# Turning layer 0's output through VectorE and DRAM, and a written order for three engines

## The chip, the cores and the metric

The kernel runs on one core of a Trainium2 chip. The metric is the device time of one execution in microseconds. A core has five engines with their own instruction streams: TensorE (PE: matmuls and transposes into PSUM; its weight loads are listed as PEld), VectorE (DVE), ScalarE (ACT), GpSimd (POOL) and SyncE (SP), which here only issues DMAs. The engines wait for one another through semaphores. A DMA's data is moved by 16 DMA engines that all issuing engines share.

## The reference

The input x has 128 graphs of 64 nodes with 256 features. Four layers follow; after each, its output is added to its input and a layer norm over the features is taken. One adjacency matrix (64 by 64) serves all graphs.

```
x = layernorm(x + L0(x))   # graph attention: Wh = x W; e = leaky(s1_i + s2_j), masked; softmax(e) Wh
x = layernorm(x + L1(x))   # GATv2 over 512 edges, 4 heads: leaky(Xq[src] + Xq[dst]) . a, softmax per src,
                           # sum of weights times Xv[dst], times W_out
x = layernorm(x + L2(x))   # normalised adjacency, two linear layers with batch norm over all rows
x = layernorm(x + L3(x))   # two graph convolutions, then four small LSTMs over windows of 1 to 4 nodes
```

The change touches layers 0 and 1 alone.

## The kernel before

**Tiling.** The 8192 rows are cut into 16 quarters (NQ) of 512 rows (QT), each of four tiles of 128 rows (PQ). A "token-major" tile has rows on the partitions, a turned one has features on the partitions; a matmul over features needs the turned one. The buffer A in SBUF has one slot of 128 by 1024 per quarter. In the old kernel it first takes layer 0's input squares, then layer 0's output (`token_major(q)`), and later layer 2's.

**Layer 0, steps per quarter.** `l0_a` gets the turned input: for quarter 0 by TensorE transposes, eight of them with two copies by ScalarE (`transposed`, lines 198 to 206), for the others by one VectorE transpose (line 220). That instruction only turns blocks of 32 by 32, so the input is loaded for it in such squares by eight DMAs of 64 KB (lines 131 to 135), with the squares at their turned places. `l0_b` projects (line 230), `l0_c` makes the scores and their exponentials (lines 241 to 252) and the reciprocal of the row sums (254), `l0_d` turns the weights, `l0_e` multiplies them with the values, adds x and takes the layer norm (lines 270 to 275): statistics on VectorE, then a power and four normalising instructions on GpSimd. The result goes into A.

**Layer 1.** `l1_t` turns that result with eight TensorE transposes (line 204) and two ScalarE copies (205). `l1_qv` makes queries and values in two halves (lines 295 to 308). `l1_graph`, eight per quarter, makes the edge sums (332) and a ReLU (334); `sums` reduces them over features (323). Two quarters share one softmax over edges (a super, S): `l1_softmax`, `l1_sums`, `l1_weights`. The last one writes the weights to a table in DRAM by four indirect DMAs from GpSimd (378), and two DMAs from SyncE load it back as dense attention matrices (384). `v_a` copies a quarter's part on GpSimd (391) and multiplies it with the values, `v_b` applies W_out, adds layer 0's result and normalises, `v_c` applies layer 2's adjacency.

**Order.** A loop over the quarters (lines 659 to 676) gives each iteration eight slots; slot b starts with `l1_graph(q, b)`, and a list `between` names the steps that follow in it. Steps of several quarters are in flight at once: layer 0 runs two quarters ahead, the values of layer 1 three or four behind. `step` ties TensorE's instructions of a step behind the last TensorE instruction of the step before (649). The order on the other engines, and on SyncE, is the planner's: it places what it takes to be ready, and each engine then works its list in order. The small set-up functions fill in during the first two iterations.

**Buffers.** Three PSUM banks named `m` serve nearly all steps; `z` has two double banks, and the head sums one.

Of the kernel before, what the change touches and what calls it, by code (L numbers as in the profile page):

```python
# [41 lines left out]
def kernel(ctx: ExitStack, tc: tile.TileContext, i, out):  # L42
# [69 lines left out]
    with ExitStack() as two:  # L112
# [13 lines left out]
        def load_x(q):  # L126
            xin[q] = xp.tile([P, PQ, D], F32, name="xin")
            nc.sync.dma_start(xin[q], x_view[q])
            if q:

                rows = i["x"][q * QT:(q + 1) * QT, :].rearrange("(j t) (k i f) -> i k t j f", t=32, k=KD, f=32)
                for n in range(4):
                    for k in range(KD):
                        to = A[n * 32:(n + 1) * 32, q, k * QT:(k + 1) * QT]
                        nc.sync.dma_start(to.rearrange("t (j f) -> t j f", f=32), rows[n, k])

        class su:

# [27 lines left out]
        for s in range(2):  # L166
            nc.sync.dma_start(bd[s * N:(s + 1) * N, s * N:(s + 1) * N], i["adj"])
        load_x(1)

        wq = wa.tile([P, KD, D + HEADS], F32, name="wq")  # L170
        wv = wa.tile([P, KD, D], F32, name="wv")
# [42 lines left out]

        def l0_a(q):
            L0[q] = {"x": xin.pop(q)}
            if q:

                L0[q]["xT"] = work.tile([P, KD, QT], F32, name="tT", bufs=1)
                nc.vector.transpose(L0[q]["xT"].rearrange("p k t -> p (k t)"), A[:, q, :])  # L220
            else:
                L0[q]["xT"] = transposed(L0[q]["x"], q)

        def l0_b(q):
            xT = L0[q]["xT"]
            wh = L0[q]["wh"] = own(q, [P, PQ, D + 2], "wh")
            for c in range(PQ):
                p_ = bank([D + 2])
                for k in range(KD):
                    nc.tensor.matmul(p_, xT[:, k, c * P:(c + 1) * P], w0[:, k, :],  # L230
                                     start=k == 0, stop=k == KD - 1)
                nc.scalar.activation(wh[:, c, :], p_, AF.Copy)

            sb = L0[q]["sb"] = own(q, [P, PQ, P], "sb")
            nc.scalar.activation(sb, wh[:, :, D + 1:].to_broadcast([P, PQ, P]), AF.Copy)

        def l0_c(q):
            wh, sb = L0[q]["wh"], L0[q]["sb"]
            sc = bank([PQ, P])
            for c in range(PQ):  # L240
                nc.tensor.transpose(sc[:, c, :], sb[:, c, :], ident)
            e = L0[q]["e"] = work.tile([P, PQ, P], F32, name="e0")
            for c in range(PQ):
                nc.vector.scalar_tensor_tensor(e[:, c, :], sc[:, c, :], wh[:, c, D:D + 1], mask,
                                               op0=OP.add, op1=OP.add)
            nc.vector.scalar_tensor_tensor(e, e, SLOPE, e, op0=OP.mult, op1=OP.max)
            mx = small.tile([P, PQ], F32, name="mx")
            nc.vector.tensor_reduce(mx, e, AX.X, OP.max, negate=True)
            sm = small.tile([P, PQ], F32, name="sm")
            for c in range(PQ):  # L250
                nc.scalar.activation(e[:, c, :], e[:, c, :], AF.Exp, bias=mx[:, c:c + 1],
                                     accum_out=sm[:, c:c + 1])
            ri = L0[q]["ri"] = small.tile([P, PQ], F32, name="ri")
            nc.vector.reciprocal(ri, sm)

        def l0_d(q):
            e = L0[q]["e"]
# [4 lines left out]
            nc.scalar.activation(eT, p_, AF.Copy)  # L262

        def l0_e(q):
            x, wh, eT, ri = (L0[q][n] for n in ("x", "wh", "eT", "ri"))
            for c2 in range(2):
                p_ = bank([2, D])
                for c in range(2):
                    g = 2 * c2 + c
                    nc.tensor.matmul(p_[:, c, :], eT[:, g, :], wh[:, g, :D], start=True, stop=True)  # L270
                for c in range(2):
                    g = 2 * c2 + c
                    nc.vector.scalar_tensor_tensor(x[:, g, :], p_[:, c, :], ri[:, g:g + 1], x[:, g, :],
                                                   op0=OP.mult, op1=OP.add)
            layernorm(token_major(q), x, PQ, nc.gpsimd)
            L0.pop(q)
            if q + 2 < NQ:
                load_x(q + 2)

# [1 line left out]
        L1 = {}  # L281

        def l1_t(q):
            L1[q] = {"xT": transposed(token_major(q)), "qs": [],
                     "v": vp.tile([P, PQ, D], F32, name="v", bufs=5)}

        def l1_qv(q, c2):
            xT, v = L1[q]["xT"], L1[q]["v"]

            sp = spads[q // BPS % 2].rearrange("p (s e x b d h) -> p s e x b d h", e=2, s=2, x=2, b=BPS, d=2)  # L290
            pv = bank([2, D])
            for c in (2 * c2, 2 * c2 + 1):
                pq = bank([D + HEADS])
                for k in range(KD):
                    nc.tensor.matmul(pq, xT[:, k, c * P:(c + 1) * P], wq[:, k, :],  # L295
                                     start=k == 0, stop=k == KD - 1)
                for k in range(KD):
                    nc.tensor.matmul(pv[:, c % 2, :], xT[:, k, c * P:(c + 1) * P], wv[:, k, :],  # L298
                                     start=k == 0, stop=k == KD - 1)

                qs = work.tile([P, 2, D], F32R, name="qs", bufs=6)
                L1[q]["qs"].append(qs)
                for s in range(2):
                    r, ro = slice(s * N, (s + 1) * N), slice((1 - s) * N, (2 - s) * N)
                    nc.scalar.activation(qs[r, s, :], pq[r, :D], AF.Copy)  # L305
                    nc.vector.tensor_sub(qs[ro, s, :], pq[r, :D], qs[r, s, :].bitcast(F32))  # L306
                    nc.scalar.activation(sp[r, s, c % 2, 0, q % BPS, c // 2, :], pq[r, D:], AF.Copy, scale=SLOPE)
            nc.scalar.activation(v[:, 2 * c2:2 * c2 + 2, :], pv, AF.Copy)
# [30 lines left out]
        def l1_softmax(S):  # L339

            pe = pes.pop(S)
            nc.tensor.matmul(pe, spads[S % 2], gath, start=False, stop=True)
            e = vp.tile([P, E], F32, name="e1")
            nc.vector.tensor_add(e, pe, lb)
            up = vp.tile([P, E], F32, name="up")
            dn = vp.tile([P, E], F32, name="dn")


            nc.vector.tensor_tensor_scan(up, seg[:, :E], e, NEG, OP.add, OP.max)
            nc.vector.tensor_tensor_scan(dn[:, ::-1], seg[:, 1:][:, ::-1], up[:, ::-1], NEG, OP.add, OP.max)  # L350
            nc.vector.tensor_sub(e, e, dn)
            nc.scalar.activation(e, e, AF.Exp)
            sm[S] = e, up, dn

        def l1_sums(S):
            e, up, dn = sm[S]
            nc.vector.tensor_tensor_scan(up, keep, e, 0.0, OP.mult, OP.add)
            nc.vector.tensor_tensor_scan(dn[:, ::-1], seg[:, 1:][:, ::-1], up[:, ::-1], NEG, OP.add, OP.max)

# [24 lines left out]
                nc.sync.dma_start(ld[S][s * N:(s + 1) * N], half)  # L384


        def v_a(q):
            S, b = divmod(q, BPS)
            v = L1[q]["v"]
            am = vp.tile([P, PQ * HEADS, N], F32, name="am")  # L390
            nc.gpsimd.tensor_copy(am.rearrange("p (e r) n -> p e r n", e=2),
                                  ld[S].rearrange("p n (e b r) -> p b e r n", e=2, b=BPS)[:, b])
            pY = [bank([KD, PQ, N]) for _ in range(2)]
            for c in range(PQ):
                for h in range(HEADS):
# [242 lines left out]
        LAG = BPS + 1  # L638


        queue = []

        def step(do, n, *more):
            if not 0 <= n < NQ:
                return
            traced = nc.cur_bb.bb.instructions
            first = len(traced)
            if queue:
                with tc.issue_after(queue[-1]):
                    do(n, *more)  # L650
            else:
                do(n, *more)
            mine = [t for t in traced[first:] if t.engine == mybir.EngineType.PE]
            queue.extend(mine[-1:])

        def sums(q):
            reduce_heads([pend.pop(0) for _ in range(min(4, len(pend)))])
# [1 line left out]
        for q in range(NQ):  # L659
            S = q // BPS - 1 if q % BPS == 0 else -1  # L660
            between = [
                [(l0_e, q + 1), (l0_a, q + 2)],
                [(sums, q if q else -1), (l1_softmax, S)],
                [(l1_sums, S), (l0_b, q + 2)],
                [(v_b, q - LAG - 1)],
                [(l1_weights, S), (l1_t, q + 1), (l0_c, q + 2)],
                [(sums, q), (l1_qv, q + 1, 0)],
                [(v_c, q - LAG - 1), (v_a, q - LAG)],
                [(l0_d, q + 2), (l1_qv, q + 1, 1)],
            ]  # L670
            for b in range(GQ):
                step(l1_graph, q, b)
# [62 lines left out]
        q = 0  # L735
        for do, n in [(v_b, NQ - LAG - 1), (v_c, NQ - LAG - 1)] + [
                (do, n) for n in range(NQ - LAG, NQ) for do in (v_a, v_b, v_c)]:
            do(n, *[False] * (do == v_c))
            up_block(q)
            q += 1  # L740
# [397 lines left out]
```

## Time and profile before

| | |
|---|---|
| Time, median of 3 runs | 2139.26 us (2139.17 to 2140.81) |
| The profiled execution | 2138.25 us, span 2136.4 us |
| TensorE, VectorE, ScalarE, GpSimd busy | 96%, 41%, 44%, 20% |
| Layers 0 and 1 in the loop | from about 53 to 522 us of the span |
| One even and the next odd iteration there | 32.7 and 28.5 us |
| TensorE transposes of layer 0's output, of the layer's 16 quarters | 128 (line 204), about 0.27 us each, overlapping |
| DMA engines' share in an odd iteration | 0.51 |

An even iteration (q even, from 2) has the three steps of a softmax in it, an odd one has not. Times in the profile are microseconds from the start of the span. A line of a timeline gives the start, the length, the engine, the source line, the instruction and its tiles, how many were merged, and in brackets how long the engine had been idle before it and what released it. Matmuls overlap their neighbours, so the cost of one is read from the start of one to the start of the next.

### The profile page before, as it was taken

How to read it: one execution, taken by the hardware profiler on the slowest of the kernel's cores; microseconds unless marked ns; L12 is line 12 of the kernel's file. 1: busy time of each engine (PE TensorE's matmuls, PEld its weight loads, DVE VectorE, ACT ScalarE, POOL GpSimd, SP SyncE). 2: the span in 40 equal slices, each digit the busy share in tenths (PEclk: the TensorE clock that was granted, in tenths of full speed). 3: DMA queues.
4: the chain of work that ended last, by engine and by line, in shares of the span. 5: the costliest groups of instructions: out<-in, count | busy, mean ns of one | idle time of the engine just before them, and what ended most of it. 6: DMA issues, size and time to landing. Idle time of an engine off the chain costs nothing.

```text
span 2136.4 us, 29441 instructions
## 1 busy us (share of the span) xinstructions
PE 2060.7 (96%) x11343; PEld 1330.1 (62%) x11343; DVE 885.9 (41%) x2069; ACT 932.1 (44%) x1795; POOL 430.1 (20%) x569
## 2 busy tenths in 40 slices
PE   5999999998999989999999999999999999999998
PEld 4666767665544444585576576577467468468467
DVE  7456566654444343333234334324324324323213
ACT  2776666664339014334234334334334334333333
POOL 1134334332210010121112112113103103102012
PEclk8999999998999989999999999999999999999999
DMA  5244532322240021012112102103103102101001
GB/s 144 63 69 73 85 61 53 52 43 43 43 118 29 0 89 60 21 54 66 40 46 74 40 29 90 40 11 99 50 6 104 50 1 89 50 1 60 20 1 60
DMA packets 232636, 113.41 MB, mean 53 GB/s; under 512 B 150192, under 2 KB 215728, under 8 KB 232240
## 3 DMA queue, kind: packets, MB, share of 16 engines
q1 hardware_dynamic: 230640, 109.57, 20.2%
q8 instruction: 89, 1.46, 0.3%
q0 software_dynamic: 1024, 1.05, 0.2%
q10 hardware_dynamic: 832, 0.92, 0.1%
q14 instruction: 51, 0.42, 0.1%
HBM read 67.45 MB, written 44.04 MB: 52 GB/s over the span
## 4 chain that ended last, share of the span: by engine, by line
PE 86%; DVE 6%; ACT 4%; issue 2%; POOL 1%; DMA 1%; SPq 0%; POOLq 0%; DVEq 0%; ACTq 0%
PE l L994 36%; PE l L1000 20%; PE pz L784 5%; PE pz L719 5%; PE e L323 3%; PE g L933 2%; PE g L945 2%; PE m L295 2%; PE m L230 2%; PE z L332 2%; PE m L298 2%; PE g L878 1%; PE m L413 1%; PE m L270 1%; ACT u L334 1%
## 5 line engine op out<-in xcount | busy, mean ns | idle before, releaser
L994 PE MATMUL l<-H,wih 128*128 128x256 f32 (+2 forms) x2496 | 787.5, 470 | 1.8 <-ACT H L957 1.2
L994 PEld LDWEIGHTS l<-H,wih 128*128 128x128 f32 x2496 | 471.4, 190 | 286.2 <-issue 185.6
L1000 PE MATMUL l<-hid,whh 128*128 128x256 f32 (+2 forms) x1536 | 435.9, 437 | 0.0
L1000 PEld LDWEIGHTS l<-hid,whh 128*128 128x128 f32 x1536 | 291.8, 190 | 128.4 <-issue 61.2
L1006 ACT ACTIVATE gate_i<-l,bias 128x256 f32<-128x256 f32 (+2 forms) x176 | 100.3, 570 | 441.9 <-PE l L1000 374.2
L1010 POOL TENSOR_TENSOR cell<-gate_f,cell 128x256 f32<-128x256 f32 (+2 forms) x96 | 85.0, 885 | 726.0 <-ACT gate_f L1006 726.0
L1009 DVE TENSOR_TENSOR gate_i<-gate_i,gate_g 128x256 f32<-128x256 f32 (+2 forms) x96 | 49.6, 517 | 415.1 <-ACT gate_g L1006 415.0
L83 POOL TENSOR_TENSOR ln_rs<-ln_rs,mhalf 128x2 f32<-128x2 f32 (+2 forms) x97 | 82.0, 846 | 571.6 <-DVE ln_rs L95 570.7
L334 ACT ACTIVATE u<-z 128x1024 f32<-128x1024 f32 x128 | 130.3, 1025 | 63.3 <-PE z L332 62.3
L1006 ACT ACTIVATE gate_g<-l,bias 128x256 f32<-128x256 f32 (+2 forms) x176 | 100.3, 570 | 107.9 <-PE l L994 59.5
L1014 ACT ACTIVATE gate_g<-cell 128x256 f32<-128x256 f32 (+2 forms) x176 | 90.0, 511 | 86.9 <-DVE cell L1013 45.0
L1013 DVE TENSOR_TENSOR cell<-gate_i,gate_g 128x512 f32<-128x512 f32 (+2 forms) x80 | 48.2, 602 | 186.5 <-ACT gate_g L1006 186.4
L1006 ACT ACTIVATE gate_o<-l,bias 128x256 f32<-128x256 f32 (+2 forms) x176 | 99.3, 564 | 59.9 <-PE l L1000 54.0
L719 PE MATMUL pz<-A,w 128*128 128x512 f32 x256 | 113.1, 595 | 0.0
L332 PE MATMUL z<-gath_r,qs 128*128 128x512 f32 x256 | 100.4, 480 | 0.7 <-ACT u L334 0.4
L306 DVE TENSOR_TENSOR qs<-m,qs 64x256 fp32r<-64x256 f32 x128 | 54.0, 422 | 107.0 <-ACT qs L305 104.8
L719 PEld LDWEIGHTS pz<-A,w 128*128 128x128 f32 x256 | 47.9, 190 | 55.3 <-issue 53.3
L295 PE MATMUL m<-wq,tT 128*128 128x260 f32 x256 | 71.8, 403 | 7.8 <-ACT yT L403 5.4
L1006 ACT ACTIVATE gate_f<-l,bias 128x256 f32<-128x256 f32 (+2 forms) x96 | 51.1, 532 | 59.6 <-PE l L1000 59.1
L1023 DVE TENSOR_TENSOR hid<-gate_o,gate_g 128x256 f32<-128x256 f32 (+2 forms) x96 | 47.4, 493 | 61.2 <-ACT gate_o L1006 35.1
L721 DVE BATCH_NORM_STATS2 st<-pz 128x6 f32<-128x512 f32 x64 | 44.4, 697 | 59.5 <-PE pz L719 59.4
L1023 DVE TENSOR_TENSOR H<-gate_o,gate_g 128x512 f32<-128x512 f32 (+1 forms) x64 | 41.3, 645 | 66.6 <-PE l L994 46.1
(242 smaller groups left out, 2525.2 us busy)
## 6 DMA issues: line engine op xcount, KB each, us to landing
way<-st SPq DMA_DIRECT2D x59, 256.0 KB
st<-way SPq DMA_DIRECT2D x236, 64.0 KB
xin<-in_x SPq DMA_DIRECT2D x16, 512.0 KB
ld<-table SPq DMA_DIRECT2D x16, 512.0 KB
x_dram<-y SPq DMA_DIRECT2D x16, 512.0 KB
x2r<-x_dram SPq DMA_DIRECT2D x32, 256.0 KB
x_dram<-A SPq DMA_DIRECT2D x64, 128.0 KB
x3r<-x_dram SPq DMA_DIRECT2D x64, 128.0 KB
```

Of the source, the lines that this page charges most:

```text
L83: nc.gpsimd.tensor_tensor(dst, dst, mhalf[:, :n], OP.pow)
L295: nc.tensor.matmul(pq, xT[:, k, c * P:(c + 1) * P], wq[:, k, :], start=k == 0, stop=k == KD - 1)
L332: nc.tensor.matmul(z[:, k, :], L1[q]["qs"][c][:, s, k * P:(k + 1) * P], gath_r, start=True, stop=True)
L334: nc.scalar.activation(u, z, AF.Relu)
L719: nc.tensor.matmul(p_, w1[:, k, m * P:(m + 1) * P], A[:, q, k * QT:(k + 1) * QT], start=k == 0, stop=k == KD - 1)
L784: nc.tensor.matmul(p_, w2[:, k, m * P:(m + 1) * P], hidden(q, k), start=k == 0, stop=k == M1 - 1)
L994: nc.tensor.matmul(gates[n], wih[p][:, k, mw * P:(mw + 1) * P], Hw[:, k, :, s, :], start=k == 0, stop=not s and k == KD - 1)
L1000: nc.tensor.matmul(gates[n], whh[p][:, k, m * P:(m + 1) * P], hid[:, k], start=False, stop=k == KD - 1)
L1006: nc.scalar.activation(act[n], gates[n], AF.Tanh if n == "g" else AF.Sigmoid, bias=bias[:, p - 1, m:m + 1])
L1010: nc.gpsimd.tensor_tensor(cell[:, j], act["f"], cell[:, j], OP.mult)
L1014: nc.scalar.activation(act["g"], cell[:, j], AF.Tanh)
L1023: nc.vector.tensor_mul(Hw[:, jj, :, s, :] if over else new[:, jj], o, t)
```

## The change

Layer 0's output is no longer turned by TensorE for quarters 2 to 15. `l0_e` writes it to a buffer in DRAM, reads it back in 32 by 32 squares with eight DMAs, and `l1_t` turns it with one VectorE transpose. Quarters 0 and 1 (`TURN = 2`) are turned by TensorE in both layers, so quarter 1's input goes back from VectorE to TensorE. The slots of A are used for more: the squares of quarter q+1's input are loaded into A once `l0_b(q)` has read what stood there, and layer 0's squares of x1 follow in the same slot.

The list of steps is new, and `step` now ties the instructions of TensorE, VectorE and GpSimd each behind the last one of the same engine in the step before. Layer 0 finishes at the end of an iteration (slot 7) and not at the start; the second half of the queries stands in slot 0 of its own quarter's iteration; the copy of the attention weights is a step of its own, `v_am`. The exponential of layer 1's softmax moves from `l1_softmax` to `l1_sums`, behind the ScalarE instructions traced by then. Layer 0's reciprocal moves from `l0_c` to `l0_e`.

```diff
+        TURN = 2
+        def load_squares(to, rows):
...
+        def load_xT(q):
+            load_squares(A[:, q, :], i["x"][q * QT:(q + 1) * QT, :])
...
         def l0_a(q):
-            if q:
-                L0[q]["xT"] = work.tile([P, KD, QT], F32, name="tT", bufs=1)
-                nc.vector.transpose(L0[q]["xT"].rearrange("p k t -> p (k t)"), A[:, q, :])
-            else:
+            if q < TURN:
                 L0[q]["xT"] = transposed(L0[q]["x"], q)
+                return
+            t = A[:, q + 1, :] if q + 1 < NQ else work.tile([P, KD * QT], F32, name="tT", bufs=1)
+            nc.vector.transpose(t, A[:, q, :])
+            L0[q]["xT"] = t.rearrange("p (k t) -> p k t", k=KD)
...
             nc.scalar.activation(sb, wh[:, :, D + 1:].to_broadcast([P, PQ, P]), AF.Copy)
+            if TURN <= q + 1 < NQ:
+                load_xT(q + 1)
...
             layernorm(token_major(q), x, PQ, nc.gpsimd)
+            if q >= TURN:
+                x1 = dram.tile([QT, D], F32, name="x1_dram", bufs=2)
+                nc.sync.dma_start(x1.rearrange("(c p) d -> p c d", p=P), token_major(q))
+                sq[q] = A[:, q + 1, :] if q + 2 < NQ else xp.tile([P, PQ, D], F32, name="xin").rearrange(
+                    "p c d -> p (c d)")
+                load_squares(sq[q], x1)
...
         def l1_t(q):
-            L1[q] = {"xT": transposed(token_major(q)), "qs": [],
...
+            xT = work.tile([P, KD, QT], F32, name="tT", bufs=1)
+            nc.vector.transpose(xT.rearrange("p k t -> p (k t)"), sq.pop(q))
...
+            with tc.issue_after([t for t in nc.cur_bb.bb.instructions if t.engine == mybir.EngineType.Activation][-1]):
+                nc.scalar.activation(e, e, AF.Exp)
...
+            for t in traced[first:]:
+                if t.engine in (mybir.EngineType.PE, mybir.EngineType.DVE, mybir.EngineType.Pool):
+                    latest[t.engine] = t
...
             between = [
-                [(l0_e, q + 1), (l0_a, q + 2)],
-                [(sums, q if q else -1), (l1_softmax, S)],
-                [(l1_sums, S), (l0_b, q + 2)],
-                [(v_b, q - LAG - 1)],
-                [(l1_weights, S), (l1_t, q + 1), (l0_c, q + 2)],
+                [(l0_e, -1 if q else 1), (l0_a, -1 if q else 2), (l1_qv, q if q else -1, 1)],
+                [(sums, q if q else -1), (l1_softmax, S), (l0_b, q + 2)],
+                [(l1_sums, S), (v_b, q - LAG - 1)],
+                [(l0_c, q + 2), (l1_t, -1 if q else 1), (v_am, q - LAG)],
+                [(l1_t, q + 1 if q else -1), (l1_weights, S)],
                 [(sums, q), (l1_qv, q + 1, 0)],
-                [(v_c, q - LAG - 1), (v_a, q - LAG)],
-                [(l0_d, q + 2), (l1_qv, q + 1, 1)],
+                [(l0_d, q + 2), (v_c, q - LAG - 1)],
+                [(v_a, q - LAG), (l0_a, q + 3 if q + 4 < NQ else -1), (l0_e, q + 2),
+                 (l0_a, q + 3 if q + 4 == NQ else -1)],
             ]
```

## The prediction

> **What bounds the kernel now.** I read the page first, then the layer 0/1 stage cut into quarter-loop iterations (the `for q` loop; I call its odd and even passes iterations), then each engine's timeline over two of them, then SyncE's and GpSimd's timelines and the DMA share in short windows.
>
> The page's first section, two of its groups, and the table by stage (columns: length; busy TensorE, weight load, VectorE, ScalarE, GpSimd; granted clock; DMA share; GB/s):
>
> ```profile
> PE 2060.7 (96%) x11343; PEld 1330.1 (62%) x11343; DVE 885.9 (41%) x2069; ACT 932.1 (44%) x1795; POOL 430.1 (20%) x569
> ...
> L204 PE MATMUL m<-ident,A 128*128 128x128 f32 x64 | 9.5, 279 | 5.4 <-ACT tT L205 2.8 <-issue 2.7
> ...
> L220 DVE STREAM_TRANSPOSE tT<-A 128x1024 f32<-128x1024 f32 x7 | 8.7, 1245 | 0.2
> ...
> 283.50:316.20 32.70, 30.23 (x276) 21.94 (x274) 23.11 (x53) 20.75 (x46) 12.55 (x14) 1.00 0.13 37
> 316.20:344.70 28.50, 27.98 (x266) 20.97 (x265) 14.32 (x43) 20.14 (x45) 10.87 (x12) 1.00 0.51 75
> ...
> 478.00:482.00 4.00, 1.64 (x10) 1.43 (x10) 3.91 (x7) 1.06 (x2) 0.36 (x1) 0.87 0.00 0
> 482.00:485.00 3.00, 2.31 (x11) 1.81 (x9) 3.00 (x11) 0.80 (x2) 0.09 (x1) 0.50 0.00 0
> ```
>
> TensorE bounds the stage: idle 2.47 us in an even iteration (q=8, with a softmax in it) and 0.52 in an odd one. The last two rows show an idle stretch being followed by half clock. Now the timelines of TensorE and VectorE in the odd iteration, then SyncE and GpSimd:
>
> ```profile
> 325.53 3.61 PE L413 MATMUL m<-wout,yT 128*128 128x256 f32 x16
> 328.80 0.82 PE L332 MATMUL z<-gath_r,qs 128*128 128x512 f32 x2
> ...
> 332.94 0.69 DVE L248 TENSOR_REDUCE mx<-e 128x4 f32<-128x512 f32 x1
> ...
> 302.29 1.09 POOL L378 DMA_INDIRECT table<-at,place  x1 [7.61 <-DVE ln_rs L95]
> ...
> 314.12 0.96 POOL L378 DMA_INDIRECT table<-at,place  x1 [2.73 <-DMA table<-at,place]
> 316.27 3.23 SPq L384 DMA_DIRECT2D ld<-table  x2
> ...
> 319.00:321.00 2.00, 2.00 (x18) 0.42 (x16) 2.00 (x7) 1.02 (x1) 0.00 (x0) 1.00 1.63 132
> ...
> 326.48 1.98 POOL L391 COPY am<-ld 128x1024 f32<-128x1024 f32 x1 [1.07 <-DMA ld<-table]
> ...
> 1014.51 0.34 SPq L863 DMA_DIRECT2D way<-st  x1
> 1016.54 2.46 SPq L865 DMA_DIRECT2D st<-way  x4
> ```
>
> See three things. VectorE finishes layer 0's scores (L248) at 333.63, that is 4.83 us after TensorE left the v_b step (L413, 328.80). The attention table takes 14.0 us from the first indirect write to the issue of its load (302.29 to 316.27), and the load 10.2 more to land (316.27 to 326.48) with the DMA engines full. The last pair is layer 3's own turn through DRAM: the reads go out 2.03 us after the write.
>
> **The Trainium skill.** VectorE: DVE Perf Modes, "The three transpose paths", says that VectorE turns 32x32 blocks only; the trace agrees in so far as L220 needs eight DMAs to place the squares first. DMA: Bandwidth & Descriptors, "Queues, rings and completion order", says that all DMAs issued by SyncE use one row of rings and that each engine takes descriptors in ring order; here the table load fills the engines from 318 to 326, and I have no case of overtaking. The same page, "Two DMAs through the same engine are not ordered", says that a DMA reading what another wrote must be issued after that one's semaphore; L865 does wait. TensorE: Matmul & The Clock Gate, "Part 1", puts the clock at half after an idle window of about 3.4 us; the 0.50 at 482 to 485, after a wait of 2.25 us and shorter ones, agrees roughly.
>
> **What is removed.** For q = 2 to 15, eight transposes (L204) and two ScalarE copies (L205, 598 ns). On TensorE, start to start, eight cost 0.88 us in the odd iteration (329.45 to 330.33), 1.30 in the even one. If every wait went too, a pair of iterations would gain 0.88 + 0.52 + 1.30 + 2.47 = 5.2 us. For ScalarE, 1.2 us per quarter is free: it is 71% busy. Quarter 1 goes back from VectorE to TensorE: eight transposes more, but the start is VectorE-bound (its L220 at 23.66 is on the chain just before the projection at 24.96), so I take a gain of 3 us (0 to 4).
>
> **What is added on VectorE.** 14 transposes of 1.25 us. VectorE is only 50 to 71% busy, but now its order is written out, and the new one stands behind layer 0's scores and in front of the query matmuls.
> Odd iteration: xT is ready 4.83 + 1.25 = 6.1 us after v_b. TensorE has in between three graph steps (0.66 each), L241 (0.4) and the sums (1.86): 4.2. It waits 1.9 us. The rest of the old iteration without transposes and wait is 28.5 - 0.88 - 0.52 = 27.1; with the 1.9, and 0.4 for layer 0's last matmuls, which now need a bank just behind v_a, 29.4 against 28.5: +0.9.
> Even iteration: VectorE's chain from the softmax's first add (289.42) to the end of the scores (305.20) is 15.8 us, and holds everything that now precedes the query matmuls' banks, the reciprocal L372 too. Add the transpose (1.25) and 0.7, since the exponential now stands behind a ReLU on ScalarE: 17.7. The softmax matmul ends 7.3 us into the new iteration (graph step 0.66, second half of queries and values 3.55 as at 341.17 to 344.72, graph step 0.66, sums 1.86, L342 0.56), so the banks are free near 25.3. About 2.3 of query and value matmuls and 6.0 for the last two slots follow: 33.6 against 32.7, so +0.9.
> The six full pairs (q = 2 to 13) thus lose 6 x 1.8 = 11 us, though 5.2 each were taken off TensorE. The ends give back: 3 at the start, 0.9 in iteration 1, 3 in iteration 14 (L204 there runs in the half clock). Sum: +4.
>
> **What is added in transfers.** Per quarter a write of 512 KB and eight reads of 64 KB in 128-byte pieces; layer 0's own eight stay but come just in time (20 us ahead of their use, hidden). x1 is ready 6.9 us after layer 0's first add (318.47 to 325.40 in the trace). With a free queue: write about 3 (2.03 for 256 KB in layer 3, so an estimate), eight issues 4.1 (0.43 to 0.58 each), landing 1.6 after the last issue (in layer 3, 936.33 to the reader's start at 937.96). That is about 15.7 us after the iteration's start, and the transpose's turn is at 18.9 (v_b ends at 14.1, plus 4.83). Hidden, with 3 us to spare, when the iteration is even.
> In front of an odd iteration it isn't free. Weights are ready about 26 into the even iteration of about 34; 14.0 later, 6 into the odd one, the table load is issued. It lands at 16.2. x1 is ready near 8.2 (its normalisation stands behind the last indirect write on GpSimd), its write is issued at 9.3 behind the load's two issues and moves its data behind the load: landed near 18.1. Reads out at 22, landed at 23.5. VectorE waits 4.6 us in its in-order queue; behind it are the query differences (L306), and TensorE waits for these. With the 1.9 above, TensorE is idle over 6 us, so the clock halves; I take 1.5 us (0 to 3.4) for it. Six times 6.1 is 36.6. I take it, since SyncE really sat before this load in the old trace, from 187.2 (its previous issue) to 193.62: the order on SyncE puts the load early.
>
> **Moved at no cost.** The reciprocal (178 ns) waits for nothing at its new place. The copy of the attention weights on GpSimd (L391, 1.99) moved a slot ahead of v_a: the table has landed by then (16.2 against 19.7). Load of x for q+2: needed a whole iteration later. Writes of x2 (2 us of DMA): their reader is layer 3.
>
> **Sum.** 4 + 36.6 = 40.6 us on the profiled span of 2136.4. The timed runs have a median of 2139.26, so I forecast 2139.3 + 40.6, near 2180 us.
>
> **Rivals.**
> 1. The transfer hides (24%). x1's write and squares pass before or between the table load's packets. For it: the odd stretch has DMA share 0.51, so there is room on average. Against: the share is 1.63 exactly while the load runs. Then +4: 2143, spread 2135 to 2153.
> 2. Faster (28%). One mechanism: TensorE keeps the 5.2 us of a pair, because the turned tile is ready before TensorE reaches the query matmuls, in slot 5. The point: VectorE must be done within 4.2 us of v_b, where I count 6.1. It needs the layer norm of v_b or the scores to start earlier than traced, for instance because v_b's second half is reached sooner. Full price: -6 x 5.2 - 7 = -38; half of it, as I think likelier, -19: 2120, spread 2101 to 2134. For it: VectorE has 14 us idle in an odd iteration (28.5 less 14.32). Against: the 4.83 us are contiguous work.
> 3. Worse (6%). The next quarter's layer 0 squares, ready 10.2 us into the iteration, are issued while SyncE waits for x1's write, and their 4.1 us of data go first: another 4.1 x 6 = 25, so 2205.
> Nothing suggests that the change would not do what it says: fourteen quarters lose L204.
>
> **How the numbers follow.** My case has 42%, its own range 2163 to 2196. Slower is 42 + 6 + 16 (of rival 1); within 0.2%, 4.3 us and about what can be told from no change, 8 of rival 1; faster 28. The range 2112 to 2198 leaves out about 7 below and 7 above.
>
> **What would show it.** L204 at 16 transposes for layer 0 and 16 for layer 1; VectorE's new transpose at about 1.25 us, waiting for the DMA of the squares for some 4 to 5 us in odd iterations and hardly in even ones; SyncE issuing x1's write behind the table load; the query matmuls (L295's successor) waiting 6 us in odd iterations, 2 to 4 in even ones; clock 0.5 after the odd waits; layers 2 and 3 unchanged in length. I am wrong if the squares land before 18.9 in odd iterations, or if the pair is under 61 us.

## The result and the profile after

| | before | after |
|---|---|---|
| Time, median | 2139.22 us (4 runs, 2138.34 to 2140.81) | 2177.14 us (4 runs, 2174.45 to 2179.53) |
| Ratio | | 1.0176, 95% interval 1.0158 to 1.0194 |
| Span of the profiled execution | 2136.4 us | 2173.8 us |

The change made the kernel 37.9 us slower. The first section of the page, the groups of the new transpose and of what is left of the old one (part of a grouped view up to 560 us), and two iterations, q=10 and q=11, as a table of windows with the columns of before:

```profile
PE 2062.7 (95%) x11239; PEld 1325.8 (61%) x11239; DVE 899.7 (41%) x2082; ACT 919.6 (42%) x1769; POOL 414.9 (19%) x569
```

```profile
L310 DVE STREAM_TRANSPOSE tT<-A 128x1024 f32<-128x1024 f32 x12 | 14.9, 1241 | 9.4 <-DMA A<-in_x 9.4
L214 PE MATMUL m<-ident,A 128*128 128x128 f32 x16 | 3.6, 350 | 0.8 <-ACT lb L639 0.8
```

```profile
375.10:409.70 34.60, 31.24 (x269) 22.32 (x267) 23.42 (x54) 19.92 (x44) 12.31 (x15) 0.95 0.34 80
409.70:440.60 30.90, 27.52 (x257) 19.95 (x256) 15.84 (x44) 19.31 (x43) 9.13 (x12) 1.00 0.68 121
...
396.00:400.00 4.00, 1.93 (x5) 1.26 (x6) 3.93 (x6) 1.72 (x9) 4.00 (x5) 0.80 0.25 99
400.00:402.00 2.00, 2.00 (x6) 1.62 (x6) 1.35 (x5) 0.85 (x3) 1.12 (x2) 0.55 0.20 74
```

The transposes are gone as announced: 16 instructions of L214 on A are left, those of quarters 0 and 1, and VectorE has 14 turns of 1.24 us (12 from A, two from another buffer). But TensorE is not less busy over the run (2062.7 us against 2060.7). The even iteration shows why: behind an idle stretch the granted clock falls to half (0.55 from 400 to 402), its mean is 0.95 instead of 1.00, and TensorE is busy for 31.24 us there instead of 30.23, with less to do. TensorE now idles 3.36 us in the even iteration and 3.38 in the odd one, where it was 2.47 and 0.52.

Its waits up to 560 us (engine, instruction, releaser: us in total, times, longest):

```profile
PE m L321 <- DVE tT L310: 34.0, 13, 5.4
PE z L358 <- ACT u L360: 6.3, 19, 1.1
...
PE m L283 <- ACT eT L273: 6.2, 3, 2.1
...
PE m L241 <- DVE A L232: 3.9, 1, 3.9
```

In the kernel before, the query matmuls (L295) wait in the loop at most 0.6 us at a time:

```profile
PE m L295 <- ACT yT L403: 5.4, 10, 0.6
```

VectorE's own wait after the change:

```profile
DVE tT L310 <- DMA A<-in_x: 9.4, 6, 4.1
```

The query matmuls (L321) wait for the turned tile 13 times, 34 us in all. VectorE in turn waits for squares only 9.4 us, so most of that wait is not the DMA's (e1 below measures it without any DMA). (The releaser is named after one of the two sets of squares, which load by the same line into A.)

The timelines of the odd iteration q=11 for TensorE and VectorE, then SyncE's queue and GpSimd around it:

```profile
420.28 3.61 PE L443 MATMUL m<-wout,yT 128*128 128x256 f32 x16
...
430.44 1.14 PE L321 MATMUL m<-wq,tT 128*128 128x260 f32 x4 [2.37 <-DVE tT L310]
```

```profile
427.69 0.69 DVE L261 TENSOR_REDUCE mx<-e 128x4 f32<-128x512 f32 x1
429.14 1.25 DVE L310 STREAM_TRANSPOSE tT<-A 128x1024 f32<-128x1024 f32 x1 [0.76 <-DMA A<-in_x]
```

```profile
411.29 4.72 SPq L412 DMA_DIRECT2D ld<-table  x2
416.24 3.70 SPq L293 DMA_DIRECT2D x_dram<-A  x1
...
423.11 4.05 SPq L138 DMA_DIRECT2D A<-x_dram  x8
```

```profile
400.26 1.09 POOL L406 DMA_INDIRECT table<-at,place  x1 [0.23 <-DVE at L402]
403.28 0.96 POOL L406 DMA_INDIRECT table<-at,place  x1 [1.93 <-DMA table<-at,place]
...
409.10 0.96 POOL L406 DMA_INDIRECT table<-at,place  x1 [1.94 <-DMA table<-at,place]
```

Read from the bottom: four indirect writes; 11.0 us after the first, the table load is issued, 1.6 us into the odd iteration; x1's write is issued behind it, at 416.24, as soon as x1 is normalised, but its issue alone takes 3.70 us; the squares are read from 423.11 and VectorE has them at 429.14, 19.4 us into the iteration. The scores (L261) end at 428.38. So the wait for squares is 0.76 us here, and TensorE, whose v_b step (L443) ended long before, waits 2.37 us for scores and turn together.

Cut into iterations (start of the first graph step to that of the next), the loss lies here:

| part | forecast | trace |
|---|---|---|
| start, up to iteration 0 | -3 | -4.1 |
| iteration 0 | 0 | +6.7 |
| iteration 1 | -0.9 | +0.9 |
| six even, 2 to 12 | +5.4 | +10.5 (0.7, then about 2 each) |
| six odd, 3 to 13 | +5.4 + 36.6 | +24.7 (8.2, 5.2, 4.3, 2.2, 2.5, 2.3) |
| iteration 14 | -3 | -3.1 |
| iteration 15 | 0 | +2.3 |
| sum | +40.5 | +37.9 |

Iteration 15 is counted up to layer 2's first matmul; the rest of the span gives back 0.5 us. The sum held, its parts did not: the even iterations lose twice what was forecast, the odd ones little more than half.

### The profile page after: what moved, and what is told of

The parts are those of the page before. It is cut to its first block, busy times and chain, and to the rows that moved or that the text cites. A ratio compares the mean times of both kernels' runs of the same rounds, so it can differ in the third digit from the quotient of the medians.

```text
span 2173.8 us, 29471 instructions
## 1 busy us (share of the span) xinstructions
PE 2062.7 (95%) x11239; PEld 1325.8 (61%) x11239; DVE 899.7 (41%) x2082; ACT 919.6 (42%) x1769; POOL 414.9 (19%) x569
## 4 chain that ended last, share of the span: by engine, by line
PE 82%; DVE 5%; DMA 4%; ACT 4%; issue 2%; SPq 1%; POOL 1%; DVEq 0%; POOLq 0%; ACTq 0%
PE l L1028 35%; PE l L1034 19%; PE pz L818 5%; PE pz L751 5%; PE g L967 2%; PE g L979 2%; PE m L321 2%; PE m L241 2%; PE m L324 2%; DMA x_dram<-A 2%; PE g L912 1%; SPq L138 1%; ACT u L360 1%; PE m L283 1%; PE e L349 1%
## 5 line engine op out<-in xcount | busy, mean ns | idle before, releaser
L321 PE MATMUL m<-wq,tT 128*128 128x260 f32 x256 | 77.1, 428 | 36.4 <-DVE tT L310 34.0
L321 PEld LDWEIGHTS m<-wq,tT 128*128 128x128 f32 x256 | 52.7, 212 | 60.0 <-DVE tT L310 46.7
L324 PE MATMUL m<-wv,tT 128*128 128x256 f32 x256 | 74.7, 419 | 1.7 <-DVE rd L400 1.2
L1057 DVE TENSOR_TENSOR hid<-gate_o,gate_g 128x256 f32<-128x256 f32 (+2 forms) x96 | 47.3, 493 | 60.9 <-ACT gate_o L1040 35.0
```

Of the source, the lines that this page charges most:

```text
L321: nc.tensor.matmul(pq, xT[k][c], wq[:, k, :], start=k == 0, stop=k == KD - 1)
L324: nc.tensor.matmul(pv[:, c % 2, :], xT[k][c], wv[:, k, :], start=k == 0, stop=k == KD - 1)
```

## The experiments

Theory: the written order on VectorE and the trip through DRAM each cost by themselves, and the trip does so because the table load is ahead of it on SyncE. Rivals: the new order costs by itself; or the DMA traffic does. Twelve kernels were run in three groups, each with runs of the kernel before on the same chip (in the last group these had a median of 2136.54 us); ratios are to those. A difference of two ratios is turned into time with 2139 us; by the intervals, such a difference is uncertain by some 4 to 5 us, so the times of iterations, read from the profiles, are given beside it.

**Taking the change apart.** Three kernels: without the trip, without trip and VectorE turn, and without the new order.

```diff
 e1_no_trip (in l0_e)
-                x1 = dram.tile([QT, D], F32, name="x1_dram", bufs=2)
...
-                load_squares(sq[q], x1)
+                sq[q] = A[:, q, :]
```

> The changed kernel without the trip through DRAM: layer 0's output is not written and not read back; VectorE turns it where it stands, so layer 1 gets blocks in the wrong places (that part of the result is left out of account). Everything else, all three written orders too, stays. Theory A (VectorE's written order carries most of the loss): the trace of the changed kernel shows VectorE waiting 9.4 us for the squares, so about 12 us come back with the clock: near 2165. Theory B (the prediction: the table load delays the squares, 36.6 us): near 2140.

Measured: 2158.54 us, ratio 1.0090 (1.0073 to 1.0107): about half of the loss came back, more than theory A had and far less than B.

```diff
 e2_order_alone (l0_e without the trip; in l1_t)
-            xT = work.tile([P, KD, QT], F32, name="tT", bufs=1)
-            nc.vector.transpose(xT.rearrange("p k t -> p (k t)"), sq.pop(q))
+            xT = transposed(token_major(q))      # all quarters on TensorE
```

> The new order of steps alone: layer 1's input is turned by eight TensorE transposes in every quarter, as before the change, and nothing is written to or read from DRAM for it. Theory A: the order costs by itself. TensorE has 0.9 us more per quarter and its banks again, VectorE 1.25 less: about as slow as the change, 2160 to 2180. Theory B: the order alone is harmless, 2135 to 2150.

Measured: 2140.05 us, ratio 1.0007 (0.9998 to 1.0016), as in theory B.

```diff
 e4_turn_alone (trip and VectorE turn kept; the list of steps as before)
+                [(l0_a, q + 2), (l0_e, q + 1)],
...
+                [(l1_weights, S), (l1_t, q + 1), (l0_c, q + 2)],
...
-                if t.engine in (mybir.EngineType.PE, mybir.EngineType.DVE, mybir.EngineType.Pool):
+                if t.engine == mybir.EngineType.PE:
```

> The other half alone: the turn through DRAM and VectorE, in the old order of steps, with TensorE's order written out and the planner's on the others. From l0_e in slot 0 to the turn in slot 4 TensorE has some 12 us of work, while the squares need about 20 from l0_e. Both theories: the squares come late in every iteration, 5 to 8 us, so 70 to 110 us slower than before: 2210 to 2250. If it is near the change or below, the order was not needed to hide the trip.

Measured: 2206.36 us, ratio 1.0314 (1.0297 to 1.0331), a little under the range. TensorE waited 60.9 us for the turn between 150 and 540 us, up to 6.6 at once.

So the new order alone is no different from before in total; with it, VectorE's turn without the trip costs 17.8 us (1.0090 less 1.0007), and the trip 18.4 more (1.0176 less 1.0090). The new order is what makes the turn bearable at all: with the old one it is 29 us worse. The waits of TensorE from 150 to 540 us in e1, in which no data came from DRAM, show that the turn costs even when the DMA is taken away:

```profile
PE m L317 <- DVE tT L306: 21.2, 11, 2.6
```

From iteration 4 on its even iterations take 34.7 to 35.1 us and its odd ones 29.7 to 29.8, against 32.9 and 28.6 in e2. In the even ones the wait is 2.6 us, and half clock follows in all five (as in the changed kernel); in the odd ones it is 1.5 us, and the clock stays full. The trip adds nothing to these even iterations; in the odd ones, 3 to 13, it adds 8.0, 4.0, 3.0, 1.0, 1.2 and 1.0 us, together 18.2.

**Layer 0's scores first.** Would the turn's place come sooner if the scores were out of its way?

```diff
 e3_scores_early
-                [(l1_sums, S), (v_b, q - LAG - 1)],
-                [(l0_c, q + 2), (l1_t, -1 if q else 1), (v_am, q - LAG)],
+                [(l0_c, q + 2), (l1_sums, S), (v_b, q - LAG - 1)],
+                [(l1_t, -1 if q else 1), (v_am, q - LAG)],
```

> The changed kernel with one step moved: layer 0's scores (l0_c) go from slot 3, between v_b and the transpose on VectorE, to the head of slot 2, before l1_sums and v_b. VectorE stands idle there for 7 us in odd iterations and 2 in even ones. Theory A: the query matmuls wait 2.6 us less in even iterations; in odd ones the squares land 19.4 us into the iteration, so the wait stays near 2: about 15 to 20 us faster than the change, 2158 to 2165. Theory B: the squares set the time in odd iterations and VectorE's order nothing: within 6 us of the change.

Measured: 2198.66 us, ratio 1.0288 (1.0271 to 1.0305), slower than the change, which neither theory had. In the even iterations the wait for the turn is gone (nearly all of the 21.8 us that remain are the odd ones'), but the weights' transposes now wait 12.2 us, 2.4 at a time, behind v_b's additions on VectorE, which the scores have pushed back. The odd iterations lose as well: the weights come later, so the table load is issued 3.8 to 5.5 us into iterations 5 to 13 instead of 1.4 to 2.3, and VectorE waits 3.1 to 5.3 us for squares behind it. The cost had moved along VectorE's queue rather than gone.

**The turn first.** The same question with the turn put ahead of the scores, without the trip, so that the data is there.

```diff
 e8_no_trip_turn_first (e1, and)
-                [(l0_c, q + 2), (l1_t, -1 if q else 1), (v_am, q - LAG)],
-                [(l1_t, q + 1 if q else -1), (l1_weights, S)],
+                [(l1_t, q + 1 if q else -1), (l0_c, q + 2), (l1_t, -1 if q else 1), (v_am, q - LAG)],
+                [(l1_weights, S)],
```

> As the kernel without the trip through DRAM (VectorE turns x1 from where it stands, so layer 1 works on a wrong layout; 2158.5 us), but quarter q+1's turn stands ahead of quarter q+2's scores in VectorE's written order. Theory (the turn costs 18.5 us because it stands behind the scores and keeps the query matmuls waiting 1.9 to 2.6 us in each iteration, with half clock after): those waits go (21.2 us before to under 6), even iterations fall from 35.1 to about 33 us and odd ones from 29.8 to 28.5: 2136 to 2143 us. Rival (VectorE is simply fuller by 1.3 us an iteration, and whatever stands last in its chain makes PE wait instead, now the scores or the weights): 2152 to 2160 us, with the wait moved to the exponents' or the weights' transposes.

Measured: 2156.95 us, ratio 1.0081 (1.0064 to 1.0097), the same as e1 within the intervals. The rival was right for the even iterations, the theory for the odd ones: from iteration 4 on these take 28.7 to 29.0 us, even ones 34.5 to 37.3. TensorE's waits, and the even iteration q=8:

```profile
PE m L320 <- DVE rd L396: 10.1, 5, 2.0
PE m L317 <- DVE e L257: 5.6, 5, 1.1
```

```profile
314.62 1.24 DVE L306 STREAM_TRANSPOSE tT<-A 128x1024 f32<-128x1024 f32 x1
...
318.28 1.75 DVE L396 RECIPROCAL rd<-m 128x256 f32<-128x256 f32 x1
```

```profile
320.09 2.93 PE L320 MATMUL m<-wv,tT 128*128 128x256 f32 x6 [2.02 <-DVE rd L396]
```

The turned tile is ready at 315.86, and the query matmuls want nothing of the scores (L257) or of the reciprocal rd; what they share with these is, by the code, only the PSUM banks `m`, which those instructions read (an inference; the trace does not name banks). VectorE works without a pause from the exponential (309.11) to 320.93, and its last steps release the banks. By this reading, whatever is last on that chain holds TensorE up. And where VectorE has room, in the odd iterations, nothing is won either: 28.7 us against 28.5 with the transposes still on TensorE.

**A VectorE instruction that nobody reads.** If the length of that chain is the cause, a turn without a reader must cost the same. It is put into the even iterations of e2.

```diff
 e10_idle_turn_even (e2, and)
+        def idle_turn(q):
+            nc.vector.transpose(A[:, q + 1, :], A[:, q, :])
-                [(l1_t, q + 1 if q else -1), (l1_weights, S)],
+                [(l1_t, q + 1 if q else -1), (idle_turn, q + 1 if S >= 0 and q + 2 < NQ else -1), (l1_weights, S)],
```

> The new order of steps alone (2140.05 us: layer 1 turned by TensorE, no trip) plus one VectorE transpose of 128 x 1024 (1.24 us) that nothing reads, at the turn's place behind the scores, in the six even iterations 2 to 12 only. Theory (even iterations are held by VectorE's chain from the softmax to the weights' reciprocal, and by the PSUM banks that its last steps give back; whatever makes it longer costs, with half clock on top; no matmul has to want the turned data): even iterations go from 32.9 to 34.7 to 35.1 us, 2150 to 2154 us, with a wait of some 2 us for the reciprocal. Rival (only the wait of the query matmuls for the turned data costs): 2140 to 2142 us.

Measured: 2151.14 us, ratio 1.0061 (1.0044 to 1.0078): 11.5 us (some 4 either way) over e2 for six instructions of 1.24 us that nobody waits for. The theory held in place and total, though not in each iteration. Waits of TensorE in e2 and in e10 between 150 and 540 us, and the iterations q=6, 7 and 8 of e10:

```profile
PE m L312 <- DVE rd L388: 3.4, 5, 0.7
```

```profile
PE m L315 <- DVE rd L391: 9.1, 5, 1.8
```

```profile
229.10:262.90 33.80, 30.84 (x277) 21.86 (x275) 23.75 (x54) 20.87 (x46) 11.73 (x14) 1.00 0.20 50
262.90:291.40 28.50, 28.07 (x265) 20.84 (x264) 14.28 (x42) 20.17 (x45) 9.79 (x13) 1.00 0.65 95
291.40:326.90 35.50, 32.55 (x277) 23.08 (x275) 23.74 (x54) 20.87 (x46) 12.71 (x15) 0.95 0.19 48
```

L312 in e2 and L315 in e10 are the same value matmuls; each of their waits grew by 1.13 us, from 0.68 to 1.81, nearly the instruction's length. The iterations 4, 6 and 10 take 33.8 us, 0.8 more than in e2, at full clock; in 8 and 12 the same wait was followed by half clock, and they take 35.4 to 35.5. Against e2, these five make 7.5 us; a wait for `am` in the last iteration (2.8 us against 0.6) is part of the rest. So a longer chain costs without anyone wanting its data; that it does so through the banks is what the code leaves, and a run with more banks was not made.

**The table load behind the squares.** Now the trip: the same transfers, in another order on SyncE.

```diff
 e5_table_late (the two DMAs leave l1_weights for a step of their own)
+        def l1_table(S):
...
+                for t in [t for t in nc.cur_bb.bb.instructions if t.engine == mybir.EngineType.SP][-9:]:
+                    order.enter_context(tc.issue_after(t))
...
+                    nc.sync.dma_start(ld[S][s * N:(s + 1) * N], half)
...
-                 (l0_a, q + 3 if q + 4 == NQ else -1)],
+                 (l0_a, q + 3 if q + 4 == NQ else -1), (l1_table, S)],
```

> The changed kernel, but the two table loads of a super-row are issued on SyncE's queue behind quarter q+2's x1 write and its eight square loads instead of ahead of them. Without the trip through DRAM this order took 2158.5 us and with it 2177.1, so the trip costs 18.6. Theory (the trip costs because the table load stands in its way: x1's write could be issued only 3.7 us late behind it and the squares landed 19.4 us into the odd iteration): most of it comes back, 2158 to 2164 us, the squares land some 14 us into the odd iteration, and VectorE's own wait for the squares (9.4 us in the changed kernel) goes under 2 us. Rival (the way write, read, land is too long by itself, or the small pieces slow everything else): 2170 us or more, VectorE still waits for the squares. Second rival (the table now comes too late for GpSimd's copy of am): VectorE's wait goes, but PE waits for am in the odd iterations, 2170 to 2185 us.

Measured: 2166.18 us, ratio 1.0129 (1.0112 to 1.0145), 10.1 us under the change and 8.3 over e1. The truth lies between the first theory and the second rival. SyncE's queue and VectorE in the odd iteration q=7, which begins at 274.5:

```profile
281.02 0.39 SPq L293 DMA_DIRECT2D x_dram<-A  x1
281.51 0.45 SPq L128 DMA_DIRECT2D xin<-in_x  x1
284.13 4.77 SPq L138 DMA_DIRECT2D A<-x_dram  x8
288.99 3.50 SPq L394 DMA_DIRECT2D ld<-table  x2
```

```profile
293.09 1.23 DVE L310 STREAM_TRANSPOSE tT<-A 128x1024 f32<-128x1024 f32 x1
```

The write's issue takes 0.39 us instead of the 3.70 of q=11 above, and the reads follow 3.1 us after it instead of 6.9. The turn no longer waits for squares there (1.5 us in the whole run), and this iteration takes 30.1 us instead of 32.8. Most of the 8.3 us left over e1 is iteration 3, the first that uses a table: v_a waits 4.6 us for `am`, since its table now comes late (31.8 us, against 24.9 in e1). In the later odd iterations 0.4 us each is left. The lateness has moved on to layer 0's own squares, now last on the queue: VectorE waits for them 3.1 to 5.4 us at the end of the odd iterations 3 to 11. Issuing the trip from another engine was not tried.

**The transfers with nobody reading them.** e2 with the trip's write and reads.

```diff
 e11_trip_unread (e2, and in l0_e)
+                nc.sync.dma_start(x1.rearrange("(c p) d -> p c d", p=P), token_major(q))
...
+                load_squares(sq[q], x1)
```

> The new order of steps alone (2140.05 us: layer 1 turned by TensorE) plus the trip's transfers, x1's write and the eight loads of squares a quarter, with nobody reading the squares. Theory (the trip costs 18.6 us only because VectorE's turn waits for squares that land late): 2140 to 2143 us. Rival (the added small pieces delay what the same queue carries for others, the layer-0 squares, the table and the x2 writes, or slow the GpSimd's table writes): 2146 to 2160 us, with new waits for am or for the layer-0 turn.

Measured: 2140.03 us, ratio 1.0016 (1.0009 to 1.0022), against 1.0007 (0.9998 to 1.0016) without them: 0.0009, or 2 us, with intervals that overlap (0 to 4 us). In the profiled executions layer 1's last graph step starts at 518.2 us, against 518.6 in e2: in sum the traffic alone cost nothing up to there. VectorE did wait for layer 0's own squares (9.2 us in five times, longest 2.4), but the iterations from 4 on are no longer than in e2.

**Both cures, and only the odd iterations.** The turn first and the table late together; then the same with the odd quarters back on TensorE.

```diff
 e9_turn_first_table_late: the edits of e8 and e5 on the changed kernel
 e12_turn_in_odd_alone (e9, and)
-            if q >= TURN:
+            if q >= TURN and q % BPS == 0:       # in l0_e: trip for even quarters alone
-            if q < TURN:
+            if q < TURN or q % BPS:              # in l1_t: odd quarters on TensorE
```

> The changed kernel with both: the turn ahead of the scores on VectorE, the table loads behind the squares on SyncE. Complete computation. Theory (two separate costs, both taken away in the even iterations; in the odd ones the squares now have to be there some 6 us earlier, about 12.5 us into the iteration, and would land at about 14): even iterations about 33 us, odd ones 29 to 31 us, 2142 to 2158 us. Rival (the odd iterations lose more than before, since scores and turn both wait for the squares): 2165 to 2185 us.

Measured: 2173.89 us, ratio 1.0156 (1.0139 to 1.0173), the same as the change within the intervals. The total lies in the rival's range, but not for its reason: from iteration 4 on the odd iterations do fall to 29.4 to 29.9 us, while the even ones take 36.2 to 38.2, with the waits of e8 (11.0 us for the reciprocal's bank, 7.1 for the scores').

> The changed kernel with the turn ahead of the scores and the table load behind the squares (2173.9 us), and odd quarters, which are turned in the even iterations, turned by TensorE as in the kernel before; the trip and VectorE's turn stay for the even quarters, in the odd iterations, where VectorE is busy half of the time. Complete computation. Theory (the whole loss of the turn itself lies in the even iterations; what is left in the odd ones is the lateness of the squares): even iterations 32.9 us, odd ones 29 to 30 us against 28.5 before, 2142 to 2149 us. Rival (the turn pays where VectorE has room, since TensorE has eight transposes less): odd iterations under 28.5 us, below 2139 us. Second rival (even iterations suffer from the odd ones' lateness): 2155 us or more.

Measured: 2153.44 us, ratio 1.0078 (1.0061 to 1.0095). Of the theory, the lengths of the steady iterations hold and the total doesn't. In the steady part (q=8 and 9):

```profile
299.70:332.30 32.60, 30.52 (x277) 21.93 (x275) 23.43 (x56) 21.01 (x46) 11.79 (x14) 1.00 0.21 53
332.30:361.70 29.40, 27.73 (x259) 19.93 (x257) 14.77 (x41) 19.22 (x43) 9.77 (x12) 1.00 0.75 128
```

Even iterations are back at e2's length, at full clock. Odd ones have 0.4 us less of TensorE's work than in e2 (27.73 against 28.17), and take 0.8 us more. The rest of the loss against e2 is early: iteration 1 takes 27.4 us instead of 25.0, iteration 3 31.1 instead of 25.1. In iteration 3 VectorE waited 9.2 us for squares that came through DRAM, in iteration 1 3.1, and TensorE 2.5 for `am`.

**A version that beats both.** In e2 iteration 0 takes 38.2 us against 28.8 before, and it has the shorter start.

```diff
 e7_order_turn2_first (e2, and)
-                [(l0_e, -1 if q else 1), (l0_a, -1 if q else 2), (l1_qv, q if q else -1, 1)],
+                [(l0_a, -1 if q else 2), (l0_e, -1 if q else 1), (l1_qv, q if q else -1, 1)],
 e13_order_free_first (e7, and)
-                if t.engine in (mybir.EngineType.PE, mybir.EngineType.DVE, mybir.EngineType.Pool):
+                if t.engine == mybir.EngineType.PE or written and t.engine in (mybir.EngineType.DVE, mybir.EngineType.Pool):
...
+            written = q > 0
```

> The new order of steps alone, all layer-1 turns on TensorE, no trip (2140.05 us), and in iteration 0 quarter 2's layer-0 turn put ahead of quarter 1's layer norm in VectorE's written order. In the order alone iteration 0 took 38.2 us against 28.8 us in the kernel before. Theory (that one place in the order costs the 9.4 us, and the shorter start of about 4 us then shows): 2131 us (2129 to 2134). Rival (iteration 0 is long for another reason, the first quarter's projections or the set-up on VectorE): 2138 to 2140 us.

Measured: 2131.70 us (11 runs), ratio 0.9966 (0.9957 to 0.9975): 7 us faster than the kernel before, as the theory had it. Iteration 0 takes 32.1 us. The wait that went is this one of e2, quarter 2's projection behind its turn, which stood behind quarter 1's layer norm on VectorE:

```profile
PE m L241 <- DVE A L232: 3.9, 1, 3.9
```

> The new order of steps alone with quarter 2's layer-0 turn first in iteration 0 (2131.7 us), and in iteration 0 the order written out for TensorE only, so that VectorE and GpSimd are free there as in the kernel before. Theory (iteration 0 still takes 32.1 us against 28.8 in the kernel before, because VectorE's written order holds the set-up there): 2127 to 2130 us. Rival (the first quarter of a start that is 4 to 6 us earlier waits for something else, a load or the set-up itself): 2131 to 2133 us.

Measured: 2130.17 us, ratio 0.9971 (0.9959 to 0.9984), not to be told from e7. Iteration 0 takes 33.5 us, so VectorE's written order was not what held it any more. Of the 4.7 us over before, 2.6 are idle time of TensorE (5.3 us against 2.7) and 2.1 busy time (28.2 us against 26.1, at a mean clock of 0.90 against 1.00). What would take them away was not tried.

## Why the prediction was right, and where its parts were not

The case (slower, the turn and the trip both making TensorE wait) was right, and so was the time (2180 forecast, 2177.1 measured). That the time came so close is luck: the odd iterations were put 17.3 us too high, and the even ones, iterations 0, 1 and 15 too low by 5.1, 6.7, 1.8 and 2.3. By its own steps:

- **What bounds the stage**: right. What is lost from iteration 2 on shows as waits of TensorE and half clock behind them: in iterations 3 to 13, which lose 34.5 us together, TensorE idles 25.9 us more than before and spends 33 us at half clock instead of none.
- **What is removed (0.88 us in an odd iteration, 1.30 in an even one)**: too high. Against e2, which has all transposes, TensorE is busy 0.55 us less in the odd iterations of e1 (27.57 against 28.12), both at full clock. In the one even iteration of e8 at full clock it is 0.7 less (30.1 against 30.8).
- **VectorE's order, odd iteration (wait 1.9 us, +0.9)**: right in kind. Without the trip (e1) the wait was 1.5 us and the odd iterations lost 1.2 (29.8 against 28.6).
- **VectorE's order, even iteration (+0.9)**: mis-sized. The chain of 17.7 us was right to a tenth (from L370 at 382.79 to the end of L402 at 400.55 is 17.76), though within it the wait for the exponential grew by 1.4 us (2.06 against 0.69) and not by 0.7. (The forecast's own sum, 7.3 and 17.7, makes 25.0 and not 25.3.) In the changed kernel the wait ahead of the query matmuls is for the turned tile, 2.58 us up to 398.07, before the chain's end; the hold-up at the chain's last steps shows in e8 and e10. And the sum had no half clock, which followed that wait. Even iterations 4 to 12 lost 2.0 each; in e10 a longer chain costs 0.8 us without half clock, near the 0.9 forecast, and 2.5 with it.
- **Collision with the table load (+36.6)**: mis-sized; the trip as a whole costs 18.4 (e1), of which the order on SyncE is 10.1 (e5). Half clock followed the waits of 5.4, 3.8 and 3.2 us in iterations 3, 5 and 7, but not those of 2.1 to 2.4 in iterations 9, 11 and 13, where the forecast counted it too. The order of issues was as foreseen (load, write, reads), and so was the slot (18.9 us forecast, 18.7 traced). But the 14.0 us from the first indirect write to the load's issue were taken over from the old trace, where a layer norm stood between the first two indirect writes on GpSimd (302.29 and 306.92) and the others came 3.5 and 3.7 us apart; written in order, all four come 2.9 to 3.0 apart, and the interval is 11.0. The squares landed 19.4 us into the iteration instead of 23.5, and VectorE waited for them 4.1, 2.2 and 1.6 us in the first three odd iterations and 0.5 to 0.8 in the later ones, where 4.6 was forecast for all. The sign of being wrong, squares before 18.9, stayed away narrowly: the earliest turn behind squares started at 19.2.
- **Ends**: start and iteration 14 right within 1.1 us. Iteration 0 was not looked at and costs 6.7: a written order of VectorE ties quarter 2's turn behind quarter 1's layer norm.
- **Costed at nothing**: the reciprocal, the writes of x2 and layer 0's own squares cause no wait of TensorE or VectorE in the changed kernel. The copy of `am` does once, in iteration 15: v_a waits 3.3 us for it, 1.4 in the kernel before, which is most of the 2.3 lost there.

Rival 1 (the transfer hides) turned out half right: in the odd iterations from 9 on, nearly so. Its total was wrong because hiding it still leaves the 18 us of e1. Rival 2 asked VectorE to be done 4.2 us after v_b; e8 gave it that in the odd iterations, where no query matmul waits for the turn any more, and they still take 28.7 us: TensorE is busy only 0.3 us less than before (27.7 against 28.0) and idle 0.5 more (1.0 against 0.5), in short waits for ScalarE. Rival 3 did happen in its order only by one DMA: a single square of layer 0's went ahead of the reads.

The Trainium skill (TensorE: Matmul & The Clock Gate, Part 1) says that activity is watched in a free-running window of about 3.4 us, so that the moment of a change of clock depends on where in the window the work falls, and that the clock is halved after an idle window of that length. The first agrees with e10, where the same wait of 1.81 us was followed by half clock in two of five iterations. The second does not: these waits, those of 2.6 us in the changed kernel and the one of 2.25 us that the prediction took for rough agreement are shorter than such a window, and here the measurement decides.

## What to carry to other kernels

Before moving work from the bounding engine to a half-idle one, look not at its busy share but at the chain in the stretch where it is busiest, and at what its last instructions release: here 1.24 us near the end of a full VectorE chain cost 0.8 us, or 2.5 with half clock, though nobody read the result; the PSUM banks that it holds back are the likely link. A wait of some 2 us ahead of TensorE is to be priced with a chance of half clock behind it: two of five at 1.8 us in e10, none of three at 2.1 to 2.4 and all eight from 2.6 up in the layer 1 waits of the changed kernel's iterations 3 to 13. For a trip through DRAM, look at what stands ahead of it in the issuing queue, and test it apart from its traffic, which here cost 0 to 4 us.

## What was not expected of the hardware

- Identical waits of 1.81 us in e10 were followed by full clock three times and by half clock twice; half clock lasted 3.4 us (the mean clock is 0.53 from 316 to 318 and 0.61 from 318 to 320, which makes 1.9 and 1.5 us at half) and cost 1.7 us. In the trace's clock record the two halvings start at 316.13 and 442.42 us, within 0.1 us of the end of their waits and 37 times 3.413 us apart. All ten stretches of half clock in that record start on one grid of this step, and so they do in the record of every other run here. The other three waits end 0.9, 0.9 and 1.8 us ahead of a step of it. That the place of a wait on this grid decides is an inference from these five.
- The issue of a single 512 KB write took 2.5 to 4.0 us on SyncE in the six odd iterations 3 to 13 of the changed kernel, behind the table load (3.70 in q=11), 0.38 us in its even iterations, and 0.38 to 0.39 us in all of e5. SyncE issued nothing else meanwhile (its next issue in q=11 is at 420.03), so what stood behind came later too.
- Four indirect writes in a row followed each other at 3.0 us, with about 1.9 us between the end of one and the start of the next. In q=8 of the kernel before, with other work among them, they were 3.5 to 4.6 us apart.
